# Expert slots by image: the first image's rows come back to x among the second image's expert tiles

## The chip, the cores and the metric

The kernel runs on one core of a Trainium2 chip. The metric is the device time of one execution in microseconds (us), as the median of several runs. A core has five engines with programs of their own: TensorE (PE, matrix products), VectorE (DVE), ScalarE (ACT), GpSimd (POOL) and SyncE (SP, which here issues most DMA transfers). Each engine works through its own program in order. Engines wait for each other by semaphores.

## The reference, and what is computed

The network takes x of shape (2, 128, 56, 56), two images of 128 channels, and applies four layers, each as x + layer(group norm of x): an agent attention, a 3x3 convolution, a mixture of experts over patches, and a bidirectional Mamba along the rows of the image. The change lies between the third and the fourth. The third layer is, cut to what matters:

```
xp = patches of 2x2 pixels of the normed x       # 2 * 784 tokens of 512 values
logits = xp @ router_w                           # 8 experts
topv, topi = top_k(softmax(logits), 2)           # two experts per token
gate = topv / sum(topv), set at topi
for e in range(8):
    val, g = split(xp @ w1[e])                   # 512 -> 2 * 1024
    out += gate[:, e] * ((val * sigmoid(g)) @ w2[e])     # 1024 -> 512
x = x + out, put back as 2x2 pixels
```

The fourth layer needs the group norm of the new x of an image before it can start on that image: a mean and a variance over 4 channels and all pixels of the image. It then computes, for a chunk of rows, a convolution of 4 taps, low-rank projections, and a scan along the row in two directions.

## The kernel before, in words

**Route** (`route`, L1030 to L1286). Every token has two assignments, one per chosen expert; there are 3136. An expert's assignments get consecutive slots, in order of the tokens, and every expert starts at a multiple of 128 slots. So a tile is 128 slots of one expert. DVE counts the assignments of each expert (`by_e`, `upto`), works out how many tiles each needs (`over`, `tiles`, `ends`, L1191 to L1200), whose weights a tile needs (`past`, `whose`, L1207 to L1216), and the slot of every assignment (`slot`, L1223 and L1229). PE turns slots into a list of token rows per tile (`inv`, L1275). The whole of it is a serial chain ahead of the first tile.

**Tiles** (`run`, L1298 to L1389). At least 25 tiles are run (`fewest`); how many more is read from the data (`more`) and chosen by a Switch (L1378). With these inputs it is three more, 28 in all. For a tile j:
- SP loads the expert's two weights w1 (4096 KB, L1314) and w2 (2048 KB, L1319), each with two buffers.
- POOL gathers the tile's 128 token rows by an indirect DMA into xr (helper `rows_of`, L1289; four buffers).
- PE transposes them (L1331) and DVE copies the result into xs_c (L1333).
- `up`: PE makes 128 matmuls into h_ps (L1342), in two halves of a gate and a value part; ACT takes the sigmoid sg (L1351), DVE the product ht (L1353).
- `down` of the tile before follows `up` of this one on PE: 16 matmuls into o_ps (L1359). ACT scales them by the gate (ot, L1361) and stores them from its own queue into os, in DRAM, at row 128 j (L1362).

**Return** (`combine`, L1391 to L1426). For each of an image's seven blocks of 112 tokens POOL gathers two rows per token out of os (g0, g1; also L1289), DVE adds them (L1415), PE transposes the sum (four matmuls, y_ps, L1418), and DVE adds it onto x (L1403, four instructions) and takes the statistics of the block (L88). The norm of the image follows (`norm_stages`, L99): statistics are put together, PE sums over groups (gn_ps, gn_ps2), ACT takes a reciprocal root by a logarithm and an exponential, DVE refines it.

**Mamba** (`mamba_pair`, L1532). `arrive(b)` (L1573) is combine and norm of image b. Image 0 arrives at L1997, alone, ahead of everything else; after its second step ACT copies a value (seen, L2001) and loads the table of the exponential and logarithm (L2002). Then comes a prologue (L2003 to L2011): the steps of the first chunk, namely pad (L1610, ACT, norm applied), conv_ps (L1705), low (L1734), dt_ps (L1759), sp_ps (L1794) and its transfers, with steps of `arrive(1)` put between them by a list of quotas. The scans (L1859) follow for the rest of the kernel. The order of all engines in this part is the order of the program's text (`manual_schedule`); in `run` a scheduler orders them.

Of the kernel before, what the change touches and what calls it, by code (L numbers as in the profile page):

```python
# [8 lines left out]
F32 = mybir.dt.float32  # L9
AF = mybir.ActivationFunctionType  # L10
ALU = mybir.AluOpType
# [4 lines left out]
EXP_LN = "natural_log_exp_and_others"  # L16
# [997 lines left out]
class PatchExperts:  # L1014
# [15 lines left out]
    def route(self, dram, wpool, conv):  # L1030
# [9 lines left out]
        with tc.tile_pool(name="l2_route", bufs=1) as one, tc.tile_pool(  # L1040
            name="l2_route_ps", bufs=2, space=PSUM
        ) as ps:
            self.fewest = -(-2 * toks // SLOTS)
            none = one.tile([SLOTS, 512], F32, name="none")
            nc.gpsimd.memset(none, 0.0)
            for j in range(self.fewest, TILES):
# [110 lines left out]
            for k, _ in enumerate(conv(1)):  # L1157
# [29 lines left out]
                ALU.add,  # L1187
            )

            over = one.tile([P, experts, most], F32, name="over")  # L1190
            nc.vector.tensor_tensor(  # L1191
                over,
                upto[:, :, nt - 1 : nt].to_broadcast([P, experts, most]),
                floor.unsqueeze(1).to_broadcast([P, experts, most]),
                ALU.is_gt,
            )
            tiles = one.tile([P, experts], F32, name="tiles")
            nc.vector.tensor_reduce(tiles, over, AX.X, ALU.add)
            ends = one.tile([P, experts], F32, name="ends")
            nc.vector.tensor_tensor_scan(ends, every_e(net, one, experts), tiles, 0.0, ALU.mult, ALU.add)  # L1200

            more = keep.tile([1, 1], I32, name="more")
            nc.vector.tensor_scalar_add(more, ends[0:1, experts - 1 : experts], -float(self.fewest))
            self.more = more

            past = one.tile([P, TILES, experts], F32, name="past")
            nc.vector.tensor_tensor(  # L1207
                past,
                ends.unsqueeze(1).to_broadcast([P, TILES, experts]),
                count_to.unsqueeze(2).to_broadcast([P, TILES, experts]),  # L1210
                ALU.is_le,
            )
            whose = one.tile([P, TILES], F32, name="whose")
            nc.vector.tensor_reduce(whose, past, AX.X, ALU.add)
            self.whose = keep.tile([P, TILES], I32, name="whose_i")
            nc.vector.tensor_scalar_min(self.whose, whose, float(experts - 1))  # L1216

            nc.vector.tensor_sub(upto, upto, by_e)
            start = one.tile([P, experts], F32, name="start")
            nc.vector.tensor_sub(start, ends, tiles)  # L1220
            nc.vector.tensor_scalar_mul(start, start, float(SLOTS))
            slot = one.tile(shape, F32, name="slot")
            nc.vector.tensor_tensor(  # L1223
                slot,
# [1 line left out]
                upto[:T].rearrange("p e n -> p n e"),  # L1226
                ALU.add,
            )
            nc.vector.tensor_tensor(slot, slot, start[:T].unsqueeze(1).to_broadcast(shape), ALU.add)  # L1229


            self.slots = []
# [62 lines left out]
            oob_is_err=False,  # L1295
        )

    def run(self, wpool, work, ps):  # L1298
# [18 lines left out]
        def down_weights(j, e):  # L1317
            w2 = downs[j % 2]
            nc.sync.dma_start(w2, w2s[e].rearrange("o k j d -> (o k) j d"))  # L1319
            return w2  # L1320

        def gather(j):
            xr = work.tile([SLOTS, 512], F32, name="xr", tag="xr", bufs=4)
            self.rows_of(xr, self.xd, self.whom[:, j : j + 1], toks)
            return xr

        def up(j, w1, xr):

            tp = ps.tile([P, 512], F32, name="xr_ps", tag="tr")
            for q in range(4):  # L1330
                nc.tensor.transpose(tp[:, q * P : (q + 1) * P], xr[:, q * P : (q + 1) * P], net.ident)  # L1331
            xc = work.tile([P, 4, SLOTS], F32, name="xs_c", tag="xs_c")
            nc.vector.tensor_copy(xc.rearrange("c q s -> c (q s)"), tp)  # L1333
            ht = work.tile([P, nj, SLOTS], F32, name="ht", tag="ht")
            for c in range(2):
                parts = []
                for part in (1, 0):
                    h_ps = ps.tile([P, 512], F32, name="h_ps", tag="h", bufs=4)
                    for i in range(4):
                        f0 = part * hidden + (4 * c + i) * P  # L1340
                        for q in range(4):
                            nc.tensor.matmul(  # L1342
                                h_ps[:, i * SLOTS : (i + 1) * SLOTS],
                                w1[:, q, f0 : f0 + P],
                                xc[:, q, :],
                                start=q == 0,
                                stop=q == 3,
                            )
                    parts.append(h_ps)
# [3 lines left out]
                nc.vector.tensor_mul(to, parts[1], sg)  # L1353
            return ht

        def down(j, ht, w2):
            o_ps = ps.tile([P, 512], F32, name="o_ps", tag="o")
            for i in range(nj):
                nc.tensor.matmul(o_ps, ht[:, i, :], w2[:, i, :], start=i == 0, stop=i == nj - 1)  # L1359
            ot = work.tile([SLOTS, 512], F32, name="ot", tag="ot")  # L1360
            nc.scalar.mul(ot, o_ps, self.share[:, j : j + 1])  # L1361
            nc.scalar.dma_start(self.os[j * SLOTS : (j + 1) * SLOTS, :], ot)  # L1362
# [4 lines left out]
        for j in range(self.fewest):  # L1367
            e = expert(j)
            w1, w2 = up_weights(j, e), down_weights(j, e)
            ht = up(j, w1, gather(j))  # L1370
            if last is not None:
                down(*last)
            last = (j, ht, w2)
        e0 = expert(self.fewest)
        first = up_weights(self.fewest, e0), down_weights(self.fewest, e0)
        xrs = {j: gather(j) for j in range(self.fewest, self.fewest + 3)}
# [11 lines left out]
                last = (j, ht, w2)  # L1388
            down(*last)  # L1389

    def combine(self, b, gathered, bank):  # L1391


        net, nc = self.net, self.net.nc
# [10 lines left out]
                )  # L1405
            net.take_stats(b, k)

        for k in range(self.nt // NB):
            t = b * self.nt // NB + k
            gs = []  # L1410
            for n in range(2):
                g = gathered(f"g{n}")
                self.rows_of(g, self.os, self.slots[n][:, t : t + 1], TILES * SLOTS)
                gs.append(g)
            nc.vector.tensor_add(gs[0], gs[0], gs[1])  # L1415
# [17 lines left out]


MAMBA_STATES, MAMBA_RANK, MAMBA_TAPS = 16, 8, 4

POOLED = {"f": (0, 1, 2, 8, 9), "b": (0, 1, 10, 11)}

# [90 lines left out]
            pads.append(pad)  # L1529


def mamba_pair(net, out, wts, combine):  # L1532

# [18 lines left out]
    with ExitStack() as ctx:  # L1552
# [14 lines left out]

        def wide_bank(name):
            return ps.tile([P, 1024], F32, name=name, tag="dA", bufs=2)

        norms = {}

        def arrive(b):  # L1573

            yield from combine(b, gathered, wide_bank)
            got = []
            for stage in net.norm_stages(b, ps_of_norms, "mm", got.append):
                fetch = stage()
                if fetch:
                    fetch()  # L1580
                yield
            mean, rstd = got[0]
            both_of = work.tile([P, 2], F32, name=f"norm{b}", tag=f"norm{b}", bufs=1)
            nc.vector.scalar_tensor_tensor(both_of[:, 0:1], mean, -1.0, rstd, ALU.mult, ALU.mult)
            nc.vector.tensor_copy(both_of[:, 1:2], rstd)
            norms[b] = (both_of[:, 1:2], both_of[:, 0:1])

        class Banks:
            def tile(self, shape, dtype, name, tag):
# [463 lines left out]
def layers(tc, a, out, wide, attention):  # L2053
    with ExitStack() as ctx:
        net = Net(ctx, tc, a)
        keep = ctx.enter_context(tc.tile_pool(name="keep2", bufs=1, side="right"))
        with tc.tile_pool(name="l1_keep", bufs=1) as taps:
# [5 lines left out]
            with tc.tile_pool(name="l2_w", bufs=2) as wpool:  # L2063
# [44 lines left out]
                with tc.tile_pool(name="l2_work", bufs=2, reuse_waits="tile") as work, tc.tile_pool(  # L2108
                    name="l2_ps", bufs=2, space=PSUM
                ) as ps:  # L2110
                    experts.run(wpool, work, ps)
        mamba_pair(net, out, wts, experts.combine)


@with_exitstack
# [33 lines left out]
```

## Time and profile before

| what | value |
|---|---|
| median of 3 runs | 3039.38 us (3038.12 to 3041.95) |
| profiled execution | 3034.5 us |
| its span | 3032.4 us |
| mean granted clock of TensorE in it | 0.945 |
| PE busy | 2681.1 us, 88% |
| DVE, ACT, POOL busy | 2182.4, 1848.6, 1472.2 us |
| up matmuls (L1342) | 3584, 407.4 us |
| down matmuls (L1359) | 448, 201.2 us |
| down weights, up weights, issue to landing | 10.7 and 20.4 us |

A line of the timeline gives start and duration in us, engine, line of the kernel, operation, output and inputs, how many, and in brackets how long the engine sat idle before it and what released it. A name with q behind the engine (SPq) is an instruction of its sequencer, which issues a transfer. A row of the windows gives the stretch, its length, the busy time of PE, PE's weight loads, DVE, ACT and POOL with the number of instructions, the granted clock of TensorE as a share of full speed, the share of time in which the DMA engines were busy, and GB/s. In the slices, each digit is a fortieth of the span, and tells tenths of busy time, or of the clock.

### The profile page before, as it was taken

What the parts mean: (1) busy time and instruction counts of PE and PEld (TensorE: products, weight loads), DVE (VectorE), ACT (ScalarE), POOL (GpSimd) and SP (SyncE); (2) the same over time, 40 slices, a digit from 0 to 9 for tenths busy, and PEclk for the clock granted to TensorE, in tenths of its full rate; (3) what the DMA queues carried; (4) which work ended last, traced back from release to release, by engine and by line L of the source; (5) the groups of instructions that cost most, each with busy time, mean ns of one, the idle gap of its engine ahead of it and who ended that gap; (6) DMA issues with size and microseconds to landing.
All of it is one profiled execution on the core that took longest, in us unless ns stands there. A gap on an engine that the chain in (4) does not pass through costs nothing. (4 is left out here: it accounts for less than half of the span.)

```text
span 3032.4 us, 39344 instructions
## 1 busy us (share of the span) xinstructions
PE 2681.1 (88%) x14924; PEld 1275.2 (42%) x14924; DVE 2182.4 (72%) x1845; ACT 1848.6 (61%) x2942; POOL 1472.2 (49%) x801
## 2 busy tenths in 40 slices
PE   7999999999998799999997678888888888888874
PEld 3333333333335688787875323333323333233321
DVE  5978998999886300100101599999999999999996
ACT  5778788788751100000000488888888888888884
POOL 3000010010422100000001689999999999999995
PEclk9999999999999799999998899999998999999987
DMA  1000000000002768787874555566555565545560
GB/s 55 1 1 1 1 1 1 1 1 1 1 1 60 271 266 327 302 323 308 316 309 165 133 122 113 120 141 137 118 117 117 113 147 123 126 115 118 123 142 29
DMA packets 157931, 369.29 MB, mean 122 GB/s; under 512 B 25156, under 2 KB 114980, under 8 KB 154132
## 3 DMA queue, kind: packets, MB, share of 16 engines
q1 hardware_dynamic: 135744, 339.30, 38.7%
q0 software_dynamic: 5520, 15.62, 1.7%
q10 hardware_dynamic: 16452, 11.61, 1.2%
q8 instruction: 121, 1.98, 0.3%
q14 instruction: 94, 0.77, 0.1%
HBM read 297.89 MB, written 17.20 MB: 104 GB/s over the span
## 5 line engine op out<-in xcount | busy, mean ns | idle before, releaser
L1840 POOL TENSOR_TENSOR dBu<-dtu,Bs 128x896 f32<-128x896 f32 x448 | 943.1, 2150 | 18.0 <-DMA dtu<-sp_u 16.0
L1859 DVE TENSOR_TENSOR_SCAN h<-dA,dBu 128x896 f32<-128x896 f32 x448 | 883.9, 2009 | 28.9 <-ACT dA L1829 21.3
L620 ACT ACTIVATE ex<-sc 128x896 f32<-128x896 f32 (+1 forms) x700 | 602.6, 918 | 125.0 <-PE sc L617 113.7
L1881 PE MATMUL y<-h,both 128*64 128x448 f32 x1792 | 467.5, 614 | 99.5 <-POOL h L1868 93.5
L627 DVE TENSOR_TENSOR ex_sum<-ex_sum,ex 128x1792 f32<-128x1792 f32 (+1 forms) x238 | 492.5, 2069 | 35.3 <-ACT ex L620 21.3
L1342 PEld LDWEIGHTS h_ps<-xs_c,w 128*128 128x128 f32 x3584 | 403.7, 192 | 19.6 <-ACT ot L1361 17.7
L1342 PE MATMUL h_ps<-xs_c,w 128*128 128x128 f32 x3584 | 407.4, 276 | 0.0
L617 PE MATMUL sc<-q,k 32*128 32x448 f32 (+1 forms) x2800 | 403.8, 588 | 3.6 <-ACT ex L620 2.9
L1870 DVE TENSOR_TENSOR h<-h,c_ps 128x1792 f32<-128x1792 f32 (+1 forms) x168 | 326.5, 1944 | 31.9 <-ACT c_ps L1847 14.9
L1353 DVE TENSOR_TENSOR ht<-h_ps,sg 128x512 f32<-128x512 f32 x56 | 38.5, 691 | 418.0 <-PE h_ps L1342 365.8
L635 PE MATMUL av<-ex,va 128*32 128x448 f32 (+1 forms) x2800 | 334.4, 552 | 0.1
L582 POOL TENSOR_TENSOR a_e<-a_e,a_inv 112x784 f32<-112x784 f32 x14 | 41.6, 2973 | 584.1 <-ACT ex L620 394.5
L1829 ACT ACTIVATE dA<-dt,f_A 128x448 f32<-128x448 f32 x448 | 282.8, 636 | 57.1 <-DVE h L1859 41.2
L1829 ACT ACTIVATE dA<-dt,b_A 128x448 f32<-128x448 f32 x448 | 282.7, 635 | 30.0 <-DVE h L1859 21.2
L1289 POOL DMA_INDIRECT xr<-xd,whom x28 | 28.1, 1003 | 519.0 <-PE xr_ps L1331 474.4
L1881 PEld LDWEIGHTS y<-h,both 128*64 128x64 f32 x1792 | 119.1, 148 | 371.1 <-issue 208.9
L1868 POOL TENSOR_TENSOR h<-h,Cs 128x1792 f32<-128x1792 f32 (+1 forms) x70 | 253.3, 3619 | 2.9 <-PE sp_ps L1794 1.9
L617 PEld LDWEIGHTS sc<-q,k 32*128 32x128 f32 (+1 forms) x2800 | 137.8, 181 | 230.1 <-issue 132.5
L1351 ACT ACTIVATE sg<-h_ps 128x512 f32<-128x512 f32 x56 | 33.4, 597 | 308.8 <-PE h_ps L1342 301.5
L1359 PE MATMUL o_ps<-w,ht 128*128 128x512 f32 x448 | 201.2, 593 | 1.2 <-DVE ht L1353 1.2
L1361 ACT ACTIVATE ot<-o_ps,share 128x512 f32<-128x512 f32 x28 | 19.2, 687 | 244.0 <-PE o_ps L1359 244.0
L625 DVE TENSOR_TENSOR ex_sum<-ex 128x1792 f32<-128x1792 f32 x56 | 114.4, 2042 | 54.6 <-ACT ex L620 54.5
(332 smaller groups left out, 2980.9 us busy)
## 6 DMA issues: line engine op xcount, KB each, us to landing
w<-in_L_conv_w_dram SPq DMA_DIRECT2D x28, 4096.0 KB, 20.4
w<-in_L_conv_w_dram SPq DMA_DIRECT2D x28, 2048.0 KB, 10.7
Bs<-far SPq DMA_DIRECT2D x56, 896.0 KB, 8.0
Cs<-far SPq DMA_DIRECT2D x448, 112.0 KB, 3.0
dtu<-sp_u SPq DMA_DIRECT2D x108, 224.0 KB, 3.9
dt<-dt SPq DMA_DIRECT2D x108, 224.0 KB, 5.1
os<-ot ACTq DMA_DIRECT2D x28, 256.0 KB, 7.9
xd<-xt SPq DMA_DIRECT2D x14, 224.0 KB, 2.7
```

The costliest lines, as they stand in the source:

```text
L617: nc.tensor.matmul(sc[:size, j, :BLK], self.m.k[rows, at : at + size], self.q[rows, :], start=True, stop=True)
L620: nc.scalar.activation(ex[:size, 2 * g : 2 * g + 2, :], sc[:size, :, :BLK], AF.Exp, scale=scale)
L627: nc.vector.tensor_add(self.total[g][:size], self.total[g][:size], ex[:size])
L635: nc.tensor.matmul(self.av[rows, :BLK], self.m.va[:size, i, rows], self.ex[i][:size, h, :], start=i == 0, stop=i == STEPS - 1,)
L1342: nc.tensor.matmul(h_ps[:, i * SLOTS : (i + 1) * SLOTS], w1[:, q, f0 : f0 + P], xc[:, q, :], start=q == 0, stop=q == 3,)
L1359: nc.tensor.matmul(o_ps, ht[:, i, :], w2[:, i, :], start=i == 0, stop=i == nj - 1)
L1829: nc.scalar.activation(self.dA[u][:, r * BLK : (r + 1) * BLK], self.dt2[:, m, r, :], AF.Exp, scale=self.w.A[:, j, 2 * m + r : 2 * m + r + 1],)
L1840: nc.gpsimd.tensor_tensor(self.dBu[u], self.dtu2[:, m], self.B[:, j, :].unsqueeze(1).to_broadcast(shape), ALU.mult)
L1859: nc.vector.tensor_tensor_scan(hf, af, bf, 0.0, ALU.mult, ALU.add)
L1868: nc.gpsimd.tensor_tensor(h4, h4, self.C[j].unsqueeze(1).to_broadcast(shape), ALU.mult)
L1870: nc.vector.tensor_tensor(h4, h4, self.c_ps[:, :BLK].unsqueeze(1).to_broadcast(shape), ALU.mult)
L1881: nc.tensor.matmul(self.y[r * H : (r + 1) * H, m, :BLK], both, self.hc[j][:, m, r, :], start=False, stop=j == PAIRS - 1)
```

## The change

Slots are given out by image and, within an image, by expert: 16 runs in place of 8. A tile in which an expert's assignments of both images meet counts for the first image, and the second image's run of this expert begins with the next tile; the number of tiles stays as it is. Of an image with 1568 assignments and eight runs the rows lie in the first (1568 + 8 x 127) // 128 = 20 tiles at most (`ahead`). So once tile 19 is stored, image 0's rows are all in os, and its gathers read only the first 20 tiles' rows of it.

`arrive` is now a function of the module. For image 0 it is run as `beside` in `run`: at tile 20 three steps (gathers of three blocks, `LEAD`), then one step at each of the spots in tiles 21 to 24, and what is left ahead of the Switch. A spot lets the step's instructions be placed only behind the matmul that was issued last. The gathered rows have four buffers (`LEAD` + 1). The norm of the image is kept. Mamba begins with the load of its ACT table and only image 1 to arrive.

The program order that results: on DVE the adds of image 0's blocks 0 to 3 stand among the two ht of tile 21, the add of block 4 ahead of xs_c of tile 22, the others in tiles 22 and 23; the norm stands behind ht of tile 24 and ahead of the Switch's branch. On POOL the gather of tile 25's rows comes first, then the 14 of image 0, in between tile 26's, then tile 27's. On PE the transposes of the blocks stand among tiles 21 to 24's matmuls, gn_ps ahead of the down matmuls of tile 23, gn_ps2 behind them. On ACT two table loads surround the logarithm of the norm, and the pad of the first chunk comes directly behind the norm, ahead of the Switch.

```
+            self.ahead = (2 * tok + experts * (SLOTS - 1)) // SLOTS
...
-            over = one.tile([P, experts, most], F32, name="over")
+            by_image = [P, NB, experts, most]
+            over = one.tile(by_image, F32, name="over")
...
-            tiles = one.tile([P, experts], F32, name="tiles")
+            tiles = one.tile([P, NB, experts], F32, name="tiles")
             nc.vector.tensor_reduce(tiles, over, AX.X, ALU.add)
+            nc.vector.tensor_sub(tiles[:, 1, :], tiles[:, 1, :], tiles[:, 0, :])
+            runs = NB * experts
+            ends = one.tile([P, runs], F32, name="ends")
...
-            past = one.tile([P, TILES, experts], F32, name="past")
+            past = one.tile([P, TILES, runs], F32, name="past")
...
+            nc.vector.tensor_scalar_min(whose, whose, float(runs - 1))
+            second = one.tile([P, TILES], F32, name="second")
+            nc.vector.tensor_scalar(second, whose, float(experts), -float(experts), ALU.is_ge, ALU.mult)
+            nc.vector.tensor_tensor(self.whose, whose, second, ALU.add)
...
+            nc.vector.tensor_scalar_mul(edge, tiles[:, 0, :], float(SLOTS))
+            nc.vector.tensor_sub(jump, start[:, experts:], start[:, :experts])
+            nc.vector.tensor_sub(jump, jump, edge)
...
+            nc.vector.tensor_tensor(later, slot, edge[:T].unsqueeze(1).to_broadcast(shape), ALU.is_ge)
+            nc.vector.tensor_tensor(later, later, jump[:T].unsqueeze(1).to_broadcast(shape), ALU.mult)
+            nc.vector.tensor_tensor(slot, slot, start[:T, :experts].unsqueeze(1).to_broadcast(shape), ALU.add)
+            nc.vector.tensor_tensor(slot, slot, later, ALU.add)
...
+        def spot():
+            with net.tc.issue_after(traced[0]):
+                next(beside, None)
...
                 nc.vector.tensor_mul(to, parts[1], sg)
+                if self.ahead + 1 < j + c < self.fewest + c:
+                    spot()
...
             last = (j, ht, w2)
+            if j == self.ahead:
+                for _ in range(LEAD):
+                    next(beside)
+            elif j > self.ahead:
+                spot()
+        for _ in beside:
+            pass
         e0 = expert(self.fewest)
...
+                rows = (self.ahead if b == 0 else TILES) * SLOTS
+                self.rows_of(g, self.os[:rows, :], self.slots[n][:, t : t + 1], rows)
...
-            for n, _ in enumerate(arrive(0)):
-                if n == 1:
-
-                    seen = work.tile([P, 1], F32, name="seen", tag="seen", bufs=1)
-                    nc.scalar.copy(seen, net.xb(0, 0)[:, 0:1])
-                    nc.scalar.preload_act_table_set(EXP_LN)
-            second = arrive(1)
+            nc.scalar.preload_act_table_set(EXP_LN)
+            second = arrive(net, combine, 1, gathered, wide_bank, ps_of_norms, keep, norms)
...
+                    first = arrive(net, experts.combine, 0, gathered, bank, Banks(), keep, norms, LEAD)
+                    experts.run(wpool, work, ps, first)
```

More of the change, by code (lines that the diff above doesn't have):

```diff
@@ L1188, in route @@
             )
-            over = one.tile([P, experts, most], F32, name="over")
+            by_image = [P, NB, experts, most]
+            over = one.tile(by_image, F32, name="over")
             nc.vector.tensor_tensor(
                 over,
-                upto[:, :, nt - 1 : nt].to_broadcast([P, experts, most]),
-                floor.unsqueeze(1).to_broadcast([P, experts, most]),
+                upto[:, :, per - 1 :: per].rearrange("p e b -> p b e").unsqueeze(3).to_broadcast(by_image),
+                floor.unsqueeze(1).unsqueeze(1).to_broadcast(by_image),
                 ALU.is_gt,
             )
-            tiles = one.tile([P, experts], F32, name="tiles")
+            tiles = one.tile([P, NB, experts], F32, name="tiles")
             nc.vector.tensor_reduce(tiles, over, AX.X, ALU.add)
-            ends = one.tile([P, experts], F32, name="ends")
-            nc.vector.tensor_tensor_scan(ends, every_e(net, one, experts), tiles, 0.0, ALU.mult, ALU.add)
+            nc.vector.tensor_sub(tiles[:, 1, :], tiles[:, 1, :], tiles[:, 0, :])
+            tiles_flat = tiles.rearrange("p b e -> p (b e)")
+            runs = NB * experts
+            ends = one.tile([P, runs], F32, name="ends")
+            nc.vector.tensor_tensor_scan(ends, every_e(net, one, runs), tiles_flat, 0.0, ALU.mult, ALU.add)
             more = keep.tile([1, 1], I32, name="more")
-            nc.vector.tensor_scalar_add(more, ends[0:1, experts - 1 : experts], -float(self.fewest))
+            nc.vector.tensor_scalar_add(more, ends[0:1, runs - 1 : runs], -float(self.fewest))
             self.more = more
-            past = one.tile([P, TILES, experts], F32, name="past")
+            past = one.tile([P, TILES, runs], F32, name="past")
             nc.vector.tensor_tensor(
                 past,
-                ends.unsqueeze(1).to_broadcast([P, TILES, experts]),
-                count_to.unsqueeze(2).to_broadcast([P, TILES, experts]),
+                ends.unsqueeze(1).to_broadcast([P, TILES, runs]),
+                count_to.unsqueeze(2).to_broadcast([P, TILES, runs]),
                 ALU.is_le,
@@ L1214, in route @@
             nc.vector.tensor_reduce(whose, past, AX.X, ALU.add)
+            nc.vector.tensor_scalar_min(whose, whose, float(runs - 1))
+            second = one.tile([P, TILES], F32, name="second")
+            nc.vector.tensor_scalar(second, whose, float(experts), -float(experts), ALU.is_ge, ALU.mult)
             self.whose = keep.tile([P, TILES], I32, name="whose_i")
-            nc.vector.tensor_scalar_min(self.whose, whose, float(experts - 1))
+            nc.vector.tensor_tensor(self.whose, whose, second, ALU.add)
             nc.vector.tensor_sub(upto, upto, by_e)
-            start = one.tile([P, experts], F32, name="start")
-            nc.vector.tensor_sub(start, ends, tiles)
+            start = one.tile([P, runs], F32, name="start")
+            nc.vector.tensor_sub(start, ends, tiles_flat)
             nc.vector.tensor_scalar_mul(start, start, float(SLOTS))
+            edge = one.tile([P, experts], F32, name="edge")
+            nc.vector.tensor_scalar_mul(edge, tiles[:, 0, :], float(SLOTS))
+            jump = one.tile([P, experts], F32, name="jump")
+            nc.vector.tensor_sub(jump, start[:, experts:], start[:, :experts])
+            nc.vector.tensor_sub(jump, jump, edge)
             slot = one.tile(shape, F32, name="slot")
@@ L1228, in route @@
             )
-            nc.vector.tensor_tensor(slot, slot, start[:T].unsqueeze(1).to_broadcast(shape), ALU.add)
+            later = one.tile(shape, F32, name="later")
+            nc.vector.tensor_tensor(later, slot, edge[:T].unsqueeze(1).to_broadcast(shape), ALU.is_ge)
+            nc.vector.tensor_tensor(later, later, jump[:T].unsqueeze(1).to_broadcast(shape), ALU.mult)
+            nc.vector.tensor_tensor(slot, slot, start[:T, :experts].unsqueeze(1).to_broadcast(shape), ALU.add)
+            nc.vector.tensor_tensor(slot, slot, later, ALU.add)
             self.slots = []
@@ L1296, in rows_of, with run @@
         )
-    def run(self, wpool, work, ps):
+    def run(self, wpool, work, ps, beside):
         net, nc, a = self.net, self.net.nc, self.net.a
@@ L1320, in down_weights @@
             return w2
+        traced = [None]
+        def spot():
+            with net.tc.issue_after(traced[0]):
+                next(beside, None)
         def gather(j):
@@ L1341, in up @@
                         for q in range(4):
-                            nc.tensor.matmul(
+                            mm = nc.tensor.matmul(
                                 h_ps[:, i * SLOTS : (i + 1) * SLOTS],
@@ L1348, in up @@
                             )
+                    traced[0] = mm.ins
                     parts.append(h_ps)
@@ L1358, in down @@
             for i in range(nj):
-                nc.tensor.matmul(o_ps, ht[:, i, :], w2[:, i, :], start=i == 0, stop=i == nj - 1)
+                mm = nc.tensor.matmul(o_ps, ht[:, i, :], w2[:, i, :], start=i == 0, stop=i == nj - 1)
+            traced[0] = mm.ins
             ot = work.tile([SLOTS, 512], F32, name="ot", tag="ot")
@@ L1389, in run, with combine @@
             down(*last)
-    def combine(self, b, gathered, bank):
+    def combine(self, b, gathered, bank, lead=0):
         net, nc = self.net, self.net.nc
@@ L1406, in onto, with fetched @@
             net.take_stats(b, k)
-        for k in range(self.nt // NB):
+        def fetched(k):
             t = b * self.nt // NB + k
@@ L1412, in combine @@
                 g = gathered(f"g{n}")
-                self.rows_of(g, self.os, self.slots[n][:, t : t + 1], TILES * SLOTS)
+                rows = (self.ahead if b == 0 else TILES) * SLOTS
+                self.rows_of(g, self.os[:rows, :], self.slots[n][:, t : t + 1], rows)
                 gs.append(g)
+            return gs
+        blocks = self.nt // NB
+        come = []
+        for k in range(min(lead, blocks)):
+            come.append(fetched(k))
+            yield
+        for k in range(blocks):
+            if k + lead < blocks:
+                come.append(fetched(k + lead))
+            gs = come.pop(0)
             nc.vector.tensor_add(gs[0], gs[0], gs[1])
@@ L1435 @@
 MAMBA_STATES, MAMBA_RANK, MAMBA_TAPS = 16, 8, 4
+LEAD = 3
 POOLED = {"f": (0, 1, 2, 8, 9), "b": (0, 1, 10, 11)}
@@ L1529, in __init__, with arrive, mamba_pair @@
             pads.append(pad)
-def mamba_pair(net, out, wts, combine):
+def arrive(net, combine, b, gathered, bank, banks, pool, norms, lead=0):
+    nc = net.nc
+    yield from combine(b, gathered, bank, lead)
+    got = []
+    for stage in net.norm_stages(b, banks, "mm", got.append):
+        fetch = stage()
+        if fetch:
+            fetch()
+        yield
+    mean, rstd = got[0]
+    both_of = pool.tile([P, 2], F32, name=f"norm{b}")
+    nc.vector.scalar_tensor_tensor(both_of[:, 0:1], mean, -1.0, rstd, ALU.mult, ALU.mult)
+    nc.vector.tensor_copy(both_of[:, 1:2], rstd)
+    norms[b] = (both_of[:, 1:2], both_of[:, 0:1])
+def mamba_pair(net, out, wts, combine, keep, norms):
     tc, nc, a = net.tc, net.nc, net.a
@@ L1569, in wide_bank @@
             return ps.tile([P, 1024], F32, name=name, tag="dA", bufs=2)
[L1571 to L1586, printed above, removed]
         class Banks:
@@ L2110, in layers, with gathered, bank, tile @@
                 ) as ps:
-                    experts.run(wpool, work, ps)
-        mamba_pair(net, out, wts, experts.combine)
+                    norms = {}
+                    def gathered(name):
+                        return work.tile([T, 512], F32, name=name, tag=name, bufs=LEAD + 1)
+                    def bank(name):
+                        return ps.tile([P, 512], F32, name=name, tag="tr")
+                    class Banks:
+                        def tile(self, shape, dtype, name, tag):
+                            return bank(name)
+                    first = arrive(net, experts.combine, 0, gathered, bank, Banks(), keep, norms, LEAD)
+                    experts.run(wpool, work, ps, first)
+        mamba_pair(net, out, wts, experts.combine, keep, norms)
 @with_exitstack
```

## The prediction

> **What bounds the kernel now.** I read the page's slices first, then busy time by windows around the change, then the timeline of the handover from experts to Mamba, then the tiles that wait there. From the slices:
> ```profile
> PE   7999999999998799999997678888888888888874
> PEclk9999999999999799999998899999998999999987
> ```
> A slice is 75.8 us; the experts fill slices 14 to 22, and then the row dips. The windows of two expert tiles, of the handover, and of Mamba's prologue:
> ```profile
> 1506.20:1528.00 21.80, 21.80 (x149) 17.64 (x148) 2.07 (x4) 1.87 (x4) 1.00 (x1) 1.00 0.81 313
> 1528.00:1549.80 21.80, 21.80 (x149) 17.64 (x148) 2.07 (x4) 1.88 (x4) 1.00 (x1) 1.00 0.82 315
> 1645.70:1677.10 31.40, 8.09 (x32) 5.72 (x32) 16.05 (x53) 1.88 (x4) 21.95 (x22) 0.52 0.54 155
> 1677.10:1714.80 37.70, 29.82 (x88) 15.60 (x88) 17.62 (x55) 15.47 (x26) 13.69 (x18) 0.90 0.71 157
> ```
> The first number is the window's length, then PE, PEld, DVE, ACT, POOL, then clock, DMA share, GB/s. An expert tile is 21.8 us of unbroken PE at clock 1.00; DVE works 2 us in it. So whatever holds PE there costs its full length. The handover is the reverse: PE works 8 of 31 us. Its timeline:
> ```profile
> 1644.95 0.69 ACT L1361 ACTIVATE ot<-o_ps,share 128x512 f32<-128x512 f32 x1 [7.29 <-PE o_ps L1359]
> ...
> 1653.71 0.69 DVE L1415 TENSOR_TENSOR g<-g,g 112x512 f32<-112x512 f32 x1 [15.40 <-DMA g<-os,at_i]
> 1656.10 0.69 DVE L1415 TENSOR_TENSOR g<-g,g 112x512 f32<-112x512 f32 x1 [1.70 <-DMA g<-os,at_i]
> 1656.71 0.81 DVE L1403 TENSOR_TENSOR x<-x,y_ps 128x112 f32<-128x112 f32 x4
> ...
> 1677.13 0.77 ACT L1610 ACTIVATE pad<-x,norm 128x448 f32<-128x448 f32 x1 [0.87 <-DVE norm L1585]
> ...
> 1677.95 7.97 PE L1705 MATMUL conv_ps<-pad,f_conv_t 128*128 128x448 f32 x16 [2.36 <-ACT pad L1610]
> ...
> 1686.61 1.28 ACT L1892 ACT_TABLE_LOAD   x1
> 1687.90 0.95 ACT L1892 ACTIVATE xc<-xc 128x896 f32<-128x896 f32 x1
> ```
> Experts end at 1644.9; image 0 is gathered, added and normed until 1677.1; only then may the convolution start. After it sp_ps (L1794) starts at 1696.00, and the first scan of Mamba at 1714.77, from where the rest runs unchanged.
>
> **The gain.** With image 0 back before the end of the experts, the prologue meets only image 1. Its gathers take image 0's place in time: first gather at 1648.74, last output row included, then adds about every 2.66 us (1653.71, ..., 1666.94 for block 5), since a gather starts every 1.30 us and a block takes two. The convolution no longer waits, which by itself would give 1677.1 - 1647.3 = 29.8 us. But in the new program order PE has the transposes of blocks 0 to 5 of image 1 ahead of sp_ps. Block 5: add 1666.94 + 0.69, transposes 0.73 to 1.6: sp_ps at 1669.2 in place of 1696.00. **-26.8 us** (-25.5 to -28.5). What follows sp_ps is the old chain.
>
> **Cost 1, route.** Sixteen runs in place of eight double the width of three DVE operations and add about ten. By rows of the same shapes (128x256 0.40, 112x112 0.32 and 0.26, small ones 0.15): wider ones 0.12+0.13+0.27+0.27, four small 0.61, two more of 128 lanes 0.30, three of 112x112 0.9. DVE is serial there, then `inv`, the row numbers and the first gather follow, and up(0) waits for that. **+2.6** (2.0 to 3.3), nothing covers it.
>
> **Cost 2, PE's own added work.** Before, the transposes of image 0 lay in PE's idle handover; now they lie in a stage without gaps. Blocks 2 to 6, 0.73 us each on a warm clock, and two small norm matmul pairs, 0.9: **+4.4** (3.5 to 5.5). Blocks 0 and 1 fall into the wait of the next step.
>
> **Cost 3, DVE's order at tiles 21 and 22.** The adds of image 0's blocks 0 to 4 stand ahead of xs_c of tile 22 in DVE's program, and up(22) needs xs_c. DVE stands at an add until its rows land; ht(21) and xs_c(22) are queued behind it, PE behind those.
> ```profile
> L1289 POOL DMA_INDIRECT xr<-xd,whom x2: 999/999/999, 1506.3 to 1528.1; - x2
> ...
> DMA to landing us min/median/max: 8.0/8.1/8.2
> ```
> ```profile
> L1289 POOL DMA_INDIRECT g<-os,at_i x22: 984/988/1340, 1648.7 to 1676.7; - x22
> ...
> DMA to landing us min/median/max: 3.3/3.4/3.7
> ```
> Both are answers for the gather's line (count, ns, starts, and from issue to landing): the first for tiles 22 and 23, while weights flow, the second for the handover. Output tile 19 is issued at 1484.53 and lands 7.9 later (section 6); POOL starts 0.8 after that: 1493.2. On POOL block 4's later gather is the twelfth: +11 x 1.30 = 1507.5. It lands at 1515.5 loaded, 1510.9 unloaded; add 0.69, two quarters onto x 0.4, xs_c 0.69: up(22) at 1517.3 or 1512.7, where it is 1506.8 now. So +10.5 or +5.9. Weights flow at that time, so I take the loaded row: **+10.5** (5.9 to 12).
>
> The Trainium skill speaks against the change here ("TensorE: Matmul & The Clock Gate", Part 1): after an idle window of about 3.4 us PE runs at half clock until about as long a stretch of work. The trace agrees: the clock fell 2.2 us after the last expert matmul (1647.15), and in the first conv the records rise 3.3 us after its start. By the rule 3.4 us at half speed lose 1.7; by the nearest row, up(0) of the first tile, 15.42 us against 14.45 of a warm one, 1.0. If DVE's waits are short, nothing. I take **+1.7** (0 to 3.4).
>
> **Cost 4, the norm ahead of the Switch.** The tiles 25 to 27 lie in a Switch (L1378). Now image 0's norm chain stands before DVE's branch. DVE's branch now:
> ```profile
> 1565.10 0.69 DVE L1353 TENSOR_TENSOR ht<-h_ps,sg 128x512 f32<-128x512 f32 x1 [6.46 <-PE h_ps L1342]
> 1571.03 0.38 SPq L1319 DMA_DIRECT2D w<-in_L_conv_w_dram  x1
> 1571.04 0.69 ACT L1361 ACTIVATE ot<-o_ps,share 128x512 f32<-128x512 f32 x1 [8.99 <-PE o_ps L1359]
> 1571.53 0.69 DVE L1333 COPY xs_c<-xr_ps 128x512 f32<-128x512 f32 x1 [5.74 <-PE xr_ps L1331]
> ```
> DVE loads `more` at 1565.13 and is ready in the branch at 1569.25: 4.1 us, hidden behind the down matmuls of tile 23, which end at E = 1570.9; xs_c follows, and up(25) starts at E + 1.3. In the new order gn_ps2 is PE's next after those matmuls, so all this comes after E: ot 0.69 on ACT, two table loads of 1.28 with 0.2 of work each, the Newton steps and the norm on DVE 0.85, the branch 4.1, xs_c 0.69, and hand-overs: up(25) at E + 9.6. ACT's own branch (6.7 us) runs beside DVE's. **+8.3** (5 to 9.5), and clock again **+1.7** (0 to 3.4). Here a rule would make it worse: "ScalarE: Activation LUTs" (What ACT_TABLE_LOAD costs) gives 1283 ns and a drain of some 1380 ns, so 5.3 us for two loads. In the trace the next activation starts 0.01 us after the load (1686.61 + 1.28, 1687.90): no drain, 2.6 us. I use the row; by the rule +2.8 more.
>
> Not costed: 14 gathers of 224 KB, 3.2 MB, move from the handover into a stage with a DMA share of 0.8; PE is late there anyway, so weights still arrive in time. At worst see the second rival. Queues: POOL has xr(25) ahead of the new gathers and xr(26) behind thirteen of them, which is needed only four tiles after up(22), at 1594 by today's times. SP issues nothing new. ACT's stores of os stand in order as before.
>
> **Sum.** -26.8 + 2.6 + 4.4 + 12.2 + 10.0 = +2.4 us. The profiled execution took 3034.5 (span 3032.4), so 3036.9 in its terms; the median of the runs is 3039.38, 4.9 above it, so **3041.8**. About 0.2% (6 us) is what a measurement of this kernel can tell from no change; this is inside.
>
> **Rivals.**
> First, the stalls stay short: gathers land as in the handover, the clock stays up, the norm chain overlaps. Low ends: 2.0 + 3.5 + 5.9 + 5 = 16.4, net -10.4, 3029. If DVE never held PE at tile 22, -16, 3023. For it: DVE has 19 of 21.8 us free, DMA a fifth. Against it: the order is fixed, and the twelfth gather can't start before 1507. Chance 0.30.
> Second, slower: the gathers queue among the weights. Twelve are open within 15 us, 2.7 MB in a stage that moves 313 GB/s, and DVE waits in order for the last. At a landing of 14 us in place of 8 the stall is 16.5: net +8.4, 3048. It decides from a landing of 11.7 us on (2.4 + 3.7 = 6.1). For it: one gather alone already rises from 3.4 to 8.0. Chance 0.29.
> Third, it doesn't do what it says: image 1's arrival holds the prologue as image 0's did, and nothing is gained: +29, 3068. The order speaks against it, since conv stands ahead of all of image 1's transposes. Chance 0.03.
> My forecast: 0.38.
>
> **Numbers.** Faster 0.30, same 0.38, slower 0.32. The range leaves 0.1 on each side: from between the two low cases, 3025, to beyond the second rival, 3052. The forecast's own range is 3034 to 3045.
>
> **What would show it.** Gain: first scan 43 us after the last o_ps, not 69.8; the conv within 5 us of it. Cost 1: up(0) at 1036.8. Cost 3: an idle DVE before the adds of tiles 21 and 22, PE idle before up(22), and the clock below 1.00 in that tile. Cost 4: two table loads before up(25), and PE idle some 8 us. Wrong if PE has no gap at these two places (then faster), or a gap over 14 us at the first (then slower).

## The result, and the profile after

The changed kernel takes 3030.35 us in the median of six runs (3024.93 to 3033.16), beside 3040.49 of the kernel before in the same session; the ratio is 0.997, with a 95% interval of 0.996 to 0.998. So it is faster by some 10 us. I had forecast 3041.8, no change that can be measured. The profiled execution took 3033.16 (span 3031.1), the slowest of its six, while that of before, 3034.5, is faster than all six timed runs of its kernel: this pair is only 1.3 us apart, so I take the traces for where time goes, and the timed runs for how much.

The slices of the profile after:

```profile
PE   7999999999998799999898778888888888888874
PEclk9999999999999799999999799899899999999987
```

PE now has its dips inside the experts, and the clock falls there to 0.7 in a slice. The windows of the changed kernel (length, then PE, PEld, DVE, ACT, POOL, clock, DMA share, GB/s): tile 21's, the wait behind it, tiles 24 and 25.

```profile
1486.40:1508.20 21.80, 14.59 (x129) 14.37 (x128) 0.00 (x0) 1.19 (x2) 8.43 (x9) 0.92 1.00 360
1508.20:1520.60 12.40, 10.45 (x28) 5.52 (x29) 6.99 (x16) 0.69 (x1) 4.78 (x5) 0.74 0.53 142
...
1570.00:1600.00 30.00, 22.48 (x153) 18.16 (x152) 2.70 (x12) 5.62 (x8) 0.00 (x0) 0.94 0.86 315
1600.00:1626.00 26.00, 23.98 (x148) 19.98 (x148) 2.70 (x4) 3.17 (x4) 0.00 (x0) 0.87 0.34 145
```

An unbroken tile had 21.8 of 21.8 us on PE. In the first of these windows PE works 14.6 and DVE nothing at all. The timelines of DVE and of PE say what they stand at:

```profile
1509.40 0.69 DVE L1461 TENSOR_TENSOR g<-g,g 112x512 f32<-112x512 f32 x1 [23.04 <-DMA g<-os,at_i]
1510.97 0.69 DVE L1461 TENSOR_TENSOR g<-g,g 112x512 f32<-112x512 f32 x1 [0.87 <-DMA g<-os,at_i]
1511.58 0.68 DVE L1377 TENSOR_TENSOR ht<-h_ps,sg 128x512 f32<-128x512 f32 x1
...
1518.02 0.69 DVE L1461 TENSOR_TENSOR g<-g,g 112x512 f32<-112x512 f32 x1 [1.96 <-DMA g<-os,at_i]
...
1519.97 0.69 DVE L1356 COPY xs_c<-xr_ps 128x512 f32<-128x512 f32 x1
```

```profile
1510.15 1.02 PE L1464 MATMUL y_ps<-ident,g 112*128 112x112 f32 x4 [9.16 <-DVE g L1461]
1510.97 8.07 PE L1385 MATMUL o_ps<-w,ht 128*128 128x512 f32 x14
```

DVE waits 23 us for the first gathered rows with ht of tile 21 behind it, and xs_c of tile 22 comes at 1519.97 instead of 1506.05. PE stands 9.2 us at the transposes of image 0's first block, ahead of the down matmuls of tile 20, which were ready. At the Switch, ACT and then PE:

```profile
1590.91 0.69 ACT L1388 ACTIVATE ot<-o_ps,share 128x512 f32<-128x512 f32 x1 [9.21 <-PE o_ps L1385]
1591.62 1.28 ACT L67 ACT_TABLE_LOAD   x1
...
1592.91 0.20 ACT L67 ACTIVATE ir_t<-ir_v 128x1 f32<-128x1 f32 x1
1593.13 1.28 ACT L68 ACT_TABLE_LOAD   x1
1594.42 0.20 ACT L68 ACTIVATE gn_rstd<-ir_t 128x1 f32<-128x1 f32 x1
```

```profile
1602.02 10.17 PE L1365 MATMUL h_ps<-xs_c,w 128*128 128x128 f32 x68 [9.03 <-issue]
```

Both stalls are there, as forecast. So is the gain, in Mamba's prologue:

```profile
1677.73 6.35 PE L1752 MATMUL conv_ps<-pad,f_conv_t 128*128 128x448 f32 x16 [0.78 <-ACT ot L1388]
...
1700.64 1.86 PE L1841 MATMUL sp_ps<-sp_e,ident 128*128 128x448 f32 x2
```

The convolution follows the last o_ps (end 1676.95) at once, sp_ps 23.7 us after it. The first scan is at 1717.74, 40.8 after the last o_ps; before it was 69.9. Added up, the changed kernel reaches the first scan **3.0 us later** than the kernel before. It is faster only in the 448 scans that follow, where the change adds, removes and reorders nothing. (What lies behind the last scan takes 2.7 us longer in this pair: 31.5 against 28.8. Over all the traces of this case it takes 28.8 to 31.5.) From the first scan to the last, the window of before, then that of after:

```profile
1714.77:3003.58 1288.81, 1057.32 (x3534) 397.41 (x3536) 1226.79 (x695) 1071.84 (x1910) 1258.15 (x584) 0.91 0.54 121
```

```profile
1717.74:2999.56 1281.82, 1069.06 (x3543) 402.23 (x3543) 1225.42 (x696) 1073.70 (x1911) 1237.54 (x584) 0.91 0.51 122
```

The stage is 7 us shorter. DVE has nearly the same busy time, POOL 21 us less with the same 584 operations, and the DMA share is lower. The group that differs on POOL, before and after (xcount, busy us, mean ns):

```profile
L1840 POOL TENSOR_TENSOR dBu<-dtu,Bs 128x896 f32<-128x896 f32 x448 | 943.1, 2150 | 18.0 <-DMA dtu<-sp_u 16.0
```

```profile
L1887 POOL TENSOR_TENSOR dBu<-dtu,Bs 128x896 f32<-128x896 f32 x448 | 921.3, 2094 | 14.4 <-DMA dtu<-sp_u 10.5
```

The same instruction takes some 50 ns less: 21.8 us of busy time over 448. (The mean falls by 56 ns, but the records of one instruction and the next overlap; a mean counts the overlap twice, the busy time once. Five in a row, before, take 10.54 us, which is 2108 ns each and not 2150.)

```profile
1904.65 10.54 POOL L1840 TENSOR_TENSOR dBu<-dtu,Bs 128x896 f32<-128x896 f32 x5
```

What could do that? In the changed kernel image 0 no longer allocates in Mamba's pools, and its norm lives in another pool. So Mamba's tiles got other addresses. In the kernel before, Bs starts at byte 112576 of each partition and dtu2 at 160960, 64 past a multiple of 128; in the changed kernel they are at 112512 and 160896, multiples of 128. h and dBu are at multiples of 128 in both. PSUM banks changed too.

### The profile page after: what moved, and what is told of

The parts are those of the page before. It is cut to its first block, busy times and chain, and to the rows that moved or that the text cites. A ratio compares the mean times of both kernels' runs of the same rounds, so it can differ in the third digit from the quotient of the medians.

```text
span 3031.1 us, 39355 instructions
## 1 busy us (share of the span) xinstructions
PE 2697.4 (89%) x14924; PEld 1283.4 (42%) x14924; DVE 2184.0 (72%) x1854; ACT 1853.7 (61%) x2944; POOL 1450.5 (48%) x801
## 5 line engine op out<-in xcount | busy, mean ns | idle before, releaser
L1887 POOL TENSOR_TENSOR dBu<-dtu,Bs 128x896 f32<-128x896 f32 x448 | 921.3, 2094 | 14.4 <-DMA dtu<-sp_u 10.5
L1906 DVE TENSOR_TENSOR_SCAN h<-dA,dBu 128x896 f32<-128x896 f32 x448 | 882.3, 2009 | 28.2 <-ACT dA L1876 24.8
L1917 DVE TENSOR_TENSOR h<-h,c_ps 128x1792 f32<-128x1792 f32 (+1 forms) x168 | 326.6, 1944 | 26.9 <-ACT c_ps L1894 10.1
L1306 POOL DMA_INDIRECT xr<-xd,whom x28 | 28.1, 1004 | 493.3 <-PE xr_ps L1354 449.3
## 6 DMA issues: line engine op xcount, KB each, us to landing
w<-in_L_conv_w_dram SPq DMA_DIRECT2D x28, 4096.0 KB, 20.4
```

The costliest lines, as they stand in the source:

```text
L1887: nc.gpsimd.tensor_tensor(self.dBu[u], self.dtu2[:, m], self.B[:, j, :].unsqueeze(1).to_broadcast(shape), ALU.mult)
L1906: nc.vector.tensor_tensor_scan(hf, af, bf, 0.0, ALU.mult, ALU.add)
L1917: nc.vector.tensor_tensor(h4, h4, self.c_ps[:, :BLK].unsqueeze(1).to_broadcast(shape), ALU.mult)
```

## The experiments

Theory A: the placing of Mamba's tiles makes the scans shorter. Theory B: the time or phase at which the stage is entered does. Theory C: it is scatter. Each kernel was timed beside the kernel before, whose medians in the four sessions were 3038.57 and 3040.02 (on one chip), 3041.11 (on a second) and 3032.12 (on a third). A ratio is to the kernel before of the same session, with its 95% interval; "scans" is the time from the first scan to the last in the one profiled execution.

**Mamba's placing alone (before_layout).**

```diff
+        ps.tile([P, 512], F32, name="first_mm", tag="mm")
+        ps.tile([P, 512], F32, name="first_c", tag="c")
+        work.tile([P, 2, BLK], F32, name="first_xc", tag="xcf", bufs=1)
...
-            both_of = work.tile([P, 2], F32, name=f"norm{b}", tag=f"norm{b}", bufs=1)
+            both_of = kept[b]
...
-                    seen = work.tile([P, 1], F32, name="seen", tag="seen", bufs=1)
+                    seen = kept[1][:, 0:1]
```

> The kernel before, with the buffers of its last stage (SBUF and PSUM) put where the changed kernel has them; no instruction is added or moved. In the profile the changed kernel reaches its first scan 3.0 us later than before, and then needs 1281.8 us to its last scan where before needs 1288.8. Theory A (placing of the buffers makes the scans' stage faster): first scan as before at about 1714.8, scans about 1282, time about 7 to 13 us under before, ratio 0.996 to 0.998. Theory B (the way in which the stage is entered, its phase, decides): scans as before, 1287 to 1295, ratio 1.000. Theory C (scatter from run to run): ratio 1.000, and the stage's length anywhere between 1280 and 1295.

Measured: ratio 0.9963 (0.995 to 0.9976), scans 1283.2, mean of dBu 2097 ns. The whole speed-up comes without the change.

**The changed kernel with the old placing (after_layout).**

```diff
+        gathered("g0")
+        gathered("g1")
+        wide_bank("first_dA")
+        work.tile([P, 1], F32, name="seen", tag="seen", bufs=1)
+        work.tile([P, 2], F32, name="first_norm", tag="norm0", bufs=1)
...
-            second = arrive(net, combine, 1, gathered, wide_bank, ps_of_norms, keep, norms)
+            second = arrive(net, combine, 1, gathered, wide_bank, ps_of_norms, work, norms)
```

> The changed kernel, with the buffers of its last stage put where the kernel before has them. Theory A (placing): scans about 1289 or more, so the time is the stage sum of +3 alone, ratio to before 1.001. Theory B (entry) and C (scatter): scans about 1280, ratio 0.997 as for the changed kernel.

Measured: 1.0019 (1.001 to 1.0027), scans 1295.5, dBu 2234 ns. With the old placing the change costs 3 to 8 us. Theories B and C fall: two kernels that enter the stage at different times follow their addresses, and both ratios are clear of 1. The two together make 0.998, beside the 0.996 to 0.998 that the change measured.

**Route alone (route_only).** The new `route` in the kernel before, image 0 returning as before.

> Slots given out by image, the rest as in the kernel before: image 0 returns in the last stage. The part of the sum for route was +2.6; the trace of the changed kernel shows tile 2 and all up to 21 later by 1.4. Expected +1.4 at the first scan. Theory A: scans as before, 1289, ratio 1.0005. Theory B: the scans may change with the entry being later by 1.4, either way. Theory C: ratio 1.0005.

Measured: 1.0012 (1.0004 to 1.002), scans 1293.9. The list of token rows (whom) comes 23.5 us after by_e instead of 21.25, so +2.3; xs_c of tile 5 is also 2.3 later after by_e here, in the changed kernel only 0.75. That stretch scatters by itself: in the kernels with the old route it is 135.3 to 136.0 us, and once 141.4. The mean of dBu is 2243 ns, more than the 2150 of the kernel before at the same addresses, but its busy time is 948.1 against 943.1: most of the difference is overlap of the records. Why they overlap more here, is open.

**PSUM or SBUF (before_psum, before_sbuf).** The two parts of before_layout: only the lines with `ps.tile`, or only the others.

> The kernel before, with only the PSUM tiles of the last stage in the changed kernel's banks (mm and c in 0 and 1, dA in 2 to 5); SBUF as before. If PSUM is what makes the scans shorter: scans 1279 to 1284, ratio 0.996. If SBUF: scans 1288 to 1295, ratio 1.000.

> The kernel before, with only the SBUF tiles of the last stage at the changed kernel's addresses; PSUM as before. If SBUF is what makes the scans shorter: scans 1279 to 1284, ratio 0.996. If PSUM: 1.000.

Measured: PSUM 0.9998 (0.9989 to 1.0006), scans 1294.9, dBu 2156 ns; SBUF 0.9968 (0.9956 to 0.9979), scans 1286.8 (2.8 more than expected), dBu 2093 ns. It is SBUF.

**Which part of SBUF (before_gap, before_xc, before_norms).**

```diff
+                    work.tile([P, 16], F32, name="gap", tag="gap", bufs=1)
                     seen = work.tile([P, 1], F32, name="seen", tag="seen", bufs=1)
```

> The kernel before with 64 unused bytes put ahead of Mamba's seen and norm tiles, nothing else. In the kernel before Bs and dtu2, the inputs of dBu, lie at 64 bytes past a multiple of 128 (112576 and 160960), in the changed kernel at multiples of 128 (112512 and 160896); h and dBu are at multiples of 128 in both. With the gap they come to 112640 and 161024, multiples of 128 at addresses that neither kernel has. If this alignment is the cause: dBu at 2.08 to 2.10 us, scans 1279 to 1287, ratio 0.996 to 0.997. If it is the particular address, or Cs and zs (still unaligned here): dBu 2.14 or more, ratio 1.000.

before_xc has only the first_xc line, before_norms only the lines of norm and seen.

> The kernel before with the convolution's output tile of the forward way placed first in Mamba's SBUF, so that it, h and dBu lie as in the changed kernel and Bs, dtu2, Cs stay where they were (64 and 96 past a multiple of 128). If the alignment of dBu's inputs is the cause: dBu 2.14 or more, ratio 1.000. If the place of h and dBu is: dBu 2.09, ratio 0.997.

> The kernel before with only the tiles seen, norm0 and norm1 taken out of Mamba's pool, so that all that lies behind them moves down by 64 or 96 bytes, onto multiples of 128; h and dBu stay. This is the part of the changed kernel that its diff shows in a line (the norms are kept in another pool). Alignment: dBu 2.09, scans 1279 to 1287, ratio 0.996 to 0.997, the same as with all SBUF tiles moved. Place of h and dBu: 1.000.

Measured: gap 0.9976 (0.9963 to 0.9989), scans 1285.9; xc 0.9996 (0.9983 to 1.001), scans 1288.6; norms 0.9958 (0.9944 to 0.9971), scans 1282.2. The group dBu in the profile with the gap, then with xc:

```profile
L1840 POOL TENSOR_TENSOR dBu<-dtu,Bs 128x896 f32<-128x896 f32 x448 | 921.5, 2093 | 15.3 <-DMA dtu<-sp_u 10.0
```

```profile
L1840 POOL TENSOR_TENSOR dBu<-dtu,Bs 128x896 f32<-128x896 f32 x448 | 943.9, 2155 | 18.2 <-DMA dtu<-sp_u 16.6
```

64 unused bytes, which put Bs and dtu2 at addresses that neither kernel has, do most of it; moving h and dBu does nothing. So it is how the tiles lie to a multiple of 128 bytes that counts, not a certain address.

**Bs alone (bs_only).** before_norms, with 64 bytes ahead of Bs and 64 behind it.

> The run without the norm tiles in Mamba's pool (all SBUF tiles of Mamba at multiples of 128, dBu 2093 ns, ratio 0.9958), with 64 unused bytes ahead of Bs and 64 behind it: Bs alone lies 64 past a multiple of 128 (at 112576, where the kernel before has it), all other tiles of the stage at multiples of 128. If the address of Bs, read by each dBu, is the cause: dBu back at 2.14 us or more and the ratio at 0.999 to 1.001. If it is that of another tile (dtu2, dt2, xc, sp_u): dBu 2.09, ratio 0.995 to 0.997. Between, 2.10 to 2.14 and 0.997 to 0.999, both inputs share it.

Measured: 1.000 (0.9989 to 1.0011), scans 1283.9, dBu 2116 ns.

```profile
L1843 POOL TENSOR_TENSOR dBu<-dtu,Bs 128x896 f32<-128x896 f32 x448 | 923.1, 2116 | 16.7 <-DMA dtu<-sp_u 12.2
```

```profile
1907.04 10.28 POOL L1843 TENSOR_TENSOR dBu<-dtu,Bs 128x896 f32<-128x896 f32 x5
```

The trace speaks against Bs alone. The mean is up by 23 ns, but that is overlap again: the busy time, 923.1 us, lies beside the 921.3 to 922.2 of the kernels with both tiles aligned and far from the 943.0 to 948.1 of the others, five in a row take 10.28, and the scans' length is among those of the aligned kernels. The ratio says the opposite, that the whole gain is lost. But it comes from the third chip, on which the kernel before took 3032.12, some 8 us less than in the other sessions, and neither a trace of it there nor an aligned kernel stands beside it. So whether the placing costs the same on that chip is not shown, and the question stays open.

**Both stalls away (both_late).** Buffers for all gathers, steps from tile 22 on, the norm behind the Switch.

```diff
-LEAD = 3
+LEAD = 7
...
-                        return work.tile([T, 512], F32, name=name, tag=name, bufs=LEAD + 1)
+                        return work.tile([T, 512], F32, name=name, tag=name, bufs=LEAD - (name == "g1"))
...
-                if self.ahead + 1 < j + c < self.fewest + c:
+                if self.ahead + 1 < j < self.fewest:
...
             nc.scalar.preload_act_table_set(EXP_LN)
+            for _ in normed(net, 0, ps_of_norms, keep, norms):
+                pass
```

> The changed kernel with both stalls taken away: all 14 gathers of image 0 into buffers of their own (7 and 6), the adds from tile 22 on, so that DVE has the rows when it comes to them; and the norm of image 0 at the start of the last stage, behind the Switch. By the stage sum: of the changed kernel's +32.0 at the last expert matmul 12.5 + 3 (tiles 22 and 23) and 10 + 2.3 (tiles 25 and 26) go, some 4 to 6 of added PE work and route stay; the convolution starts some 8 us later behind the norm, of which 3 to 5 reach the first scan. First scan 18 to 24 us ahead of the kernel before, time 0.990 to 0.994 with scans as before, 0.986 to 0.991 with scans as in the changed kernel. If the stalls are not what costs, 0.997.

Measured: 0.9972 (0.9962 to 0.9981), a miss: 0.986 to 0.991 was expected with such scans (1279.5). The norm's part was right: tile 25 takes 22.6 us instead of 31.9, and the first scan follows the last o_ps by 43.9 instead of 40.8. But the adds still stood ahead of ht of tile 21, since a spot holds back only PE's instructions, and not all of the step's as the section on the change has it; DVE now stood there for all seven blocks, and xs_c of tile 22 came 43.4 us after that of tile 21:

```profile
1514.13 0.69 DVE L1461 TENSOR_TENSOR g<-g,g 112x512 f32<-112x512 f32 x1 [23.20 <-DMA g<-os,at_i]
...
1532.99 0.69 DVE L1461 TENSOR_TENSOR g<-g,g 112x512 f32<-112x512 f32 x1 [7.05 <-DMA g<-os,at_i]
1533.60 0.68 DVE L1356 COPY xs_c<-xr_ps 128x512 f32<-128x512 f32 x1
```

**DVE's order (adds_held).** The same buffers and start, the norm as in the change, and:

```diff
-            with net.tc.issue_after(traced[0]):
+            with net.tc.issue_after(traced[0]), net.tc.issue_after(product[0]):
...
-                nc.vector.tensor_mul(to, parts[1], sg)
+                product[0] = nc.vector.tensor_mul(to, parts[1], sg).ins
```

> The changed kernel with buffers for all gathers of image 0 (7 and 6), the steps from tile 22 on, and DVE's adds held behind the last ht in program order, as the transposes are behind the last matmul. In the run with both stalls moved, DVE still stood at the adds ahead of ht of tile 21, since only PE's instructions were held. Expected if DVE's place in its order is the cause of the stall: tiles 22 and 23 lose only PE's added work, 4 to 5 us in all, instead of 18.2 in tiles 22 to 24; tile 25 keeps its 10 and tile 26 its 2.3. Last expert matmul 18 us later than in the kernel before instead of 32, time 0.992 to 0.994 with the scans of the changed kernel. If the gathers themselves slow the weights, tiles 22 and 23 stay long and the ratio stays at 0.997.

Measured: 0.9947 (0.9933 to 0.9962), a little less gain than expected. Tile 22's step, from xs_c to xs_c, is the plain 21.8; tiles 23 to 25 take 24.6, 28.2 and 32.7. The last o_ps is 22 us later than before, counted from by_e, instead of 31. The stall was the place of the adds in DVE's order. A new wait took part of it: PE stood 4.0 us for weights. Of the weights asked for at 1504.89 and 1505.46, among the gathers, w2 landed after 18.3 us and w1 after 28.1, where 10.7 and 20.4 are usual.

**The norm ahead (norm_early).** As adds_held, with up to three steps at a spot, so that gn_ps2 comes in tile 24.

> As the run with held adds, and two steps at some places, so that the norm's last matmul comes in tile 24 ahead of the down matmuls of tile 23 and its chain on ACT and DVE runs beside PE. Expected: tile 25 at 22 to 24 us instead of 31.9, last expert matmul 6 to 9 us later than before, first scan 20 to 24 us ahead of before; time 0.988 to 0.991 with the scans of the changed kernel. If the Switch and not the norm is what costs, tile 25 stays at about 30.

Measured: 3011.39, ratio 0.9902 (0.9885 to 0.9919), as expected and the fastest of all; first scan at 1694.44, 20.3 us ahead of before, scans 1285.3, dBu 2092 ns. Tile 24 and the first tile of the Switch, and PE's waits:

```profile
1558.80:1580.90 22.10, 22.10 (x151) 17.86 (x150) 2.75 (x9) 6.90 (x9) 0.00 (x0) 1.00 0.76 300
1580.90:1602.70 21.80, 21.76 (x149) 17.64 (x148) 2.08 (x3) 1.88 (x3) 0.00 (x0) 1.00 0.80 302
```

```profile
PE h_ps L1368 <- DMA w<-in_L_conv_w_dram: 2.9, 2, 2.1
```

PE runs through at clock 1.00: the Switch costs nothing once the norm is done in time.

## Why the prediction was wrong, point by point

| step | forecast | measured |
|---|---|---|
| gain, from the last o_ps | -26.8 | -27.4 at sp_ps (51.1 to 23.7), -29.1 at the first scan (69.9 to 40.8) |
| route | +2.6 | +2.3 at whom, +0.75 left at tile 5 |
| DVE's order, tile 22 | +10.5 | +12.5 (step of xs_c 34.3, was 21.8) |
| PE's added work, clock of tile 22 | +4.4 +1.7 | +5.7 (steps of tiles 23 and 24, 25.3 and 24.1) |
| norm ahead of the Switch, tile 25 | +8.3 | +10.0 (31.9, was 21.9) |
| clock, tile 26 | +1.7 | +2.3 (24.15) |
| at the first scan | +2.4 | +2.3 from by_e, +3.0 from the start |
| scans | 0 | -7.0 in this pair |
| behind the last scan | 0 | +2.7 in this pair |
| sum | +2.4 | -1.3 in this pair; -10.1 by the medians |

The sum for everything that the change does stands, to the first scan, though some of its terms are right by luck (below). **The step that failed is a single clause: "the first scan of Mamba at 1714.77, from where the rest runs unchanged".** It put the scans at nothing, without a reason; the new placing alone makes the kernel faster by 0.37% (before_layout), 11 us. The instructions are unchanged, their addresses are not. The four profiles in which Bs and dtu2 lie at 64 past a multiple of 128, besides that of before (after_layout, route_only, before_psum, before_xc), have scans of 1288.6 to 1295.5; those in which both are aligned have 1279.5 to 1286.8. On the average of the traces that is 8.9 us; with the +2.3 ahead of the scans it makes -6.6, near the edge of what the ratio allows (some -6 to -12). That kernels with aligned tiles are faster by 7 to 13 us and those without are not is shown, in the first three sessions; through which tile, and whether POOL's longer dBu or the slower transfers (DMA share 0.53 to 0.54 against 0.50 to 0.52) hold the scans, is not. DVE, which makes the scans, is busy for 95% or more of the stage in both traces of the pair; of its waits the one for ACT's copies of c_ps shrinks most, from 14.9 to 10.1 us, and what holds ACT there was not followed.

The gain came out as its working says, with two remarks. The 1647.3 in it is the reading of no view: with the order changed, the convolution starts 0.8 us after the last o_ps instead of 33.0, so by itself it gained 32.3. And the way from the last o_ps to the first scan is 68.0 to 71.6 us in the other kernels that return image 0 there, so 1.7 us between sp_ps and the scan are within its scatter.

The first rival's time, 3029, is the one measured, but not by its mechanism: the stalls did not stay short. The second rival's mechanism was there: the first eight gathers, issued from 1494.65 to 1503.73, landed from 1508.69 to 1513.30, 9.6 to 14.0 us after their issue, where 8 was forecast. w1's transfer, issued at 1485.79, landed at 1508.89. Of all fourteen:

```profile
DMA to landing us min/median/max: 3.3/10.5/14.0
```

I had missed something else beside it: g0 and g1 have four buffers each, so POOL could start no ninth gather between 1503.73 and 1510.37, until DVE's adds freed them. The twelfth, block 4's later one, started at 1514.51 instead of 1507.5, but the weights were through by then and it landed in 3.4 us instead of 8, at 1517.93 instead of 1515.5. Two errors of opposite signs left +12.5 near +10.5: that is luck. The path was longer than forecast, too: at the end DVE waits 0.8 us for PE, which had stood at block 0's transposes and came to tile 22's own only behind the delayed down matmuls. "Blocks 0 and 1 fall into the wait of the next step" overlooked that PE stands at block 0 in its own order.

The +5.7 is near its forecast by luck as well. (Its terms, 5 x 0.73 and 0.9, make 4.55, not 4.4.) PE waited 1.9 us ahead of tile 23's transposes for a PSUM bank that these share with y_ps; DVE, standing until 1542.31 at block 6's add, read y_ps late. Then the clock was at half for 3.4 us. By an estimate from these two, 1.9 and 1.7, some 2.1 us are left for the added matmuls.

What I left uncosted, gathers among weights, costs 2.9 to 4.0 us of PE once the stalls are gone. Of the two rules weighed, the clock's held in kind, but not in size. PE stopped at 1500.99 and at 1592.99, and its clock fell 3.5 and 3.7 us later (2.2 in the prediction's reading of the kernel before). When PE went on, it worked 4.6 and 4.9 us at half clock, which by an estimate loses 2.3 and 2.5 where 1.7 was forecast. The first loss falls inside the +12.5; for the second, tile 26 lost 2.3. The second stretch:

```profile
1596.69:1606.93 10.24, 4.91 (x23) 4.94 (x24) 0.69 (x1) 0.00 (x0) 0.00 (x0) 0.50 1.04 404
```

The clock was at half from 1545.49 to 1548.90 too, behind PE's wait of only 1.9 us, which the forecast did not have. The drain behind a table load did not show: the next activation starts 0.01 us after it (1591.62 + 1.28, 1592.91).

## What to carry to other kernels

When a change moves a tile from one pool to another, look at the addresses of all that lies behind it, and compare the busy time of the same instructions, before and after, in the stages that the change does not touch. Work that is moved into a stage bound by one engine costs no more than its own instructions there only if no engine of that stage stands in order at its transfers; here it took holding it behind the stage's own instructions on DVE as well as on PE, and doing the norm a tile before the branch, and even then PE waited 2.9 us for weights.

## What was not expected of the hardware

POOL's 448 f32 products dBu (128x896) took 921.3 to 922.2 us of busy time, 2056 to 2059 ns each, with Bs and dtu2 at multiples of 128 bytes, and 943.0 to 948.1 us, 2105 to 2116 ns each, with both 64 bytes past one; with Bs alone so, 923.1 us. The means of the records, 2091 to 2097, 2150 to 2243 and 2116 ns, differ more, since the records overlap. A transfer of dt took 4.9 us in the kernels with both aligned, and in bs_only, and 5.1 in the five others.
